# Gather or pair: 186 instead of 144 edge chunks of a graph layer built from an on-chip table, earlier and with larger offset loads

## The chip, the cores and the metric

The kernel runs on one core of one Trainium2 chip. The metric is the device time of one execution in microseconds; lower is better.

## What is computed

One layer of a graph network with a residual, all float32: N = 12500 nodes of D = 128 features, E = 200000 edges sorted by destination, H = 512.

```python
edge_index = jnp.stack([src, dst])
h = jnp.maximum(_layernorm(x, axis=-1), 0.0)
x = x + _L0_gnn_ref(h, edge_index, ...)
# _L0_gnn_ref(z, edge_index, ...):
msgs = z[src]
agg = jax.ops.segment_sum(msgs, dst, num_segments=n)
deg = jax.ops.segment_sum(jnp.ones((src.shape[0],), z.dtype), dst, num_segments=n)
agg = agg / jnp.maximum(deg, 1.0)[:, None]
h = jax.nn.relu(agg @ Wg + z @ Ws + bg)
h = jnp.tanh(h @ W1 + b1)
h = jnp.tanh(h @ W2 + b2)
return h @ W3 + b3
```

## The kernel before

**Set-up** (lines 282 to 400). The function that runs is `windowed`; `general` is a fallback for other graphs. x comes in pieces of ten tiles of 128 rows. Each piece is normalised: VectorE (DVE) sums and centres, ScalarE (ACT) squares (L270) and takes the root (L276), DVE scales (L280) into a tile `h`, and SP stores it to the row table `htab` in memory. In between, src and dst are turned by TensorE (PE) into columns (L340): `scol` holds the row numbers to gather, `dloc` the places of the destinations. `places` keeps, for every fourth chunk, the addresses of the rows of its 128 edges in a second table.

**Chunks.** The edges are 1563 chunks of 128. A chunk's 128 rows of h are multiplied by a one-hot matrix (L540 on DVE, for eight chunks at once, five buffers) and added into PSUM by PE (`add`, L695). The rows come in three ways:

- 80 chunks in ten groups are *raw*: POOL gathers rows of x (L217) before `htab` is there, and DVE normalises them (`centre`, four operations of 128x1024 a group) between the one-hots of the first hundred chunks.
- Most come by a *gather* of `htab`, one indirect DMA on POOL a chunk (L451), into a ring of 26 tiles (`AHEAD`).
- Of every fourth chunk some are made *by pairs* from a table on chip. `tab` (128 x 12544) holds h turned, one column a node. A chunk takes 64 operations, each of which reads two columns, whose places stand in registers, and writes their sum and the second of them (the one-hot is made to fit, L547). `lanes[0]` does this on ACT (L491, reported as L518), `lanes[1]` on DVE (L500). The offsets come into registers by a load (L461, TENSOR_LOAD) of `LOADS` = 16 numbers, that is eight pairs. PE then transposes the finished columns (`turn`, L505) and ACT copies them to a tile `turned`, which is added like a gathered one.

**`tab`** is filled in the loop: for each block of 512 nodes SP loads `htab` back (`own`, L746), PE transposes four tiles, ACT copies them into `tab` (`own_turned`, L754), one block every two chunks, 25 in all.

**Order.** PE, ACT and SP work in the order in which the program is written (`keep_in_program_order`); DVE's one-hots and pairs are placed by the same loop over chunks (L934). Its clock is `behind`, the number of gathered chunks added so far. `load_times` (L887) puts the pairs of a chunk on ACT 28 gathers ahead of its use, on DVE 36; `turns` (L901) puts transpose and copy 14 ahead. So everything that ACT does at a place in the loop that depends on PE waits until PE is there. The one-hot of a group of eight is written two groups ahead. The matrix layers of a finished block (512 nodes) are spread over the chunks that follow (`go_on`); from chunk 1312 on (`QUICK`) they follow a plan of when each gather lands.

**Which chunks.** `SHARES` = 72, 72 chunks for ACT and DVE are spread evenly over the slots (every fourth chunk from the fourth on) from `FROM` = 80 up to `ENDS` = 1480 and 1540. 1563 - 80 - 144 = 1339 chunks are gathered.

Of the kernel before, what the change touches and what calls it, by code (L numbers as in the profile page):

```python
# [22 lines left out]
F32 = mybir.dt.float32  # L23
# [8 lines left out]
P = 128  # L32
EPS = 1e-5
CPR = 16
BLK = 512
# [10 lines left out]
BEHIND = 2  # L46
EVERY = 4
AT = 3
SHARES = 72, 72
FROM, ENDS = 80, (1480, 1540)  # L50
MARGIN = 28
SUMS_AT, BANK = 1 << 25, 2048
AHEAD_OF_USE = 2
EDGE_BANK = 7
TOGETHER = 4
LOADS = 16

# [23 lines left out]
def windowed(ctx, tc, x, src, dst, Wg, Ws, bg, W1, b1, W2, b2, W3, b3, out, flag):  # L81
    nc = tc.nc
    N, D = x.shape
# [57 lines left out]
    blocks, n = [], 0  # L141
# [46 lines left out]
    ps_m = ctx.enter_context(tc.tile_pool(name="ps_m", bufs=4, space=PSUM))  # L188
# [5 lines left out]
    for t, a in ((rsrc, src), (rdst, dst)):  # L194
        a = a[RAW0 * P : RAW1 * P].rearrange("(u e) -> u e", u=NRAW)[:, : GRP * P]
# [18 lines left out]
    for g in range(NRAW):  # L214
        t = raws.tile([P, GRP, D], F32, name=f"raw{g}")
# [7 lines left out]
    ident = const.tile([P, P], F32, name="ident")  # L223
# [41 lines left out]
    def centre(pool, xt, k, stats, bufs=2):  # L265
        nc.vector.tensor_reduce(stats[:, 0], xt, AX.X, ALU.add)
        nc.vector.scalar_tensor_tensor(xt, spread(stats[:, 0], k), -1.0 / D, xt, op0=ALU.mult, op1=ALU.add)  # L267
        sq = (pool.tile([P, PIECE, D], F32, name="sq") if bufs > 1 else pool.tile([P, GRP, W_RAW], F32, name="ohr", bufs=1)[:, :, :D])[:, :k]
        if bufs > 1:
            nc.scalar.activation(sq, xt, AF.Square)  # L270
        else:
            nc.vector.tensor_tensor(sq, xt, xt, op=ALU.mult)
        nc.vector.tensor_reduce(stats[:, 1], sq, AX.X, ALU.add)
# [8 lines left out]
    with tc.tile_pool(name="ln", bufs=2) as ln:  # L282
# [80 lines left out]
        for i, (t0, k) in enumerate(pieces):  # L363
            xt = ln.tile([P, PIECE, D], F32, name="xt", bufs=3)
            whole = min(N - t0 * P, k * P) // P
            rest = min(N - t0 * P, k * P) - whole * P
            if rest:
                nc.vector.memset(xt[:, whole, :], 0.0)
            nc.sync.dma_start(xt[:, :whole, :], x[t0 * P : (t0 + whole) * P, :].rearrange("(t p) d -> p t d", p=P))
            if rest:  # L370
                nc.sync.dma_start(xt[:rest, whole, :], x[(t0 + whole) * P : N, :])
            if i == 1:
                indices("src", src, 0, keep_src)
            stats = ps_a.tile([P, BLK], F32, name="agg")[:, : 2 * k].rearrange("p (s t) -> p s t", s=2)
            xt = xt[:, :k]
            centre(ln, xt, k, stats)
            factors(stats)
            h = ln.tile([P, PIECE, D], F32, name="h", bufs=2)
            scale(h[:, :k], xt, k, stats)
            nc.sync.dma_start(htab[t0 * P : (t0 + k) * P, :].rearrange("(t p) d -> p t d", p=P), h[:, :k])  # L380


        number = sp.tile([NROW, CPR], F32, name="number")
# [50 lines left out]
    ml = ctx.enter_context(tc.tile_pool(name="ml", bufs=2))  # L434
# [11 lines left out]
    def sp_dma(*a):  # L446
        tc.keep_in_program_order(nc.sync.dma_start(*a))
# [10 lines left out]
    def offsets(lane, c, p0):  # L458
        r, q = divmod(c, CPR)
        kind = (mybir.EngineType.Activation, mybir.EngineType.DVE)[lane]  # L460
        loads, vs = nc.values_load_multi_w_load_instructions(  # L461
            places[r : r + 1, q // EVERY, p0 : p0 + LOADS], engines=[kind], min_val=TAB_AT,
            max_val=TAB_AT + (N - 1) * 4,
# [14 lines left out]
    def two(lane, c, p0):  # L478

        by_pair = columns[c].rearrange("p (t i) -> p i t", t=2)  # L480
        at_v = dict(offsets(lane, c, p0))
        for p in range(p0, p0 + LOADS, 2):
            a, b = (tab[:, bass.ds((at_v[q] - TAB_AT) // 4, 1)] for q in (p, p + 1))
            yield p, by_pair[:, p // 2], a, b

    def column_copies():
        for c in lanes[0]:
            columns[c] = ed.tile([P, P], F32, name="cols1", bufs=4)
            for p0 in range(0, P, LOADS):
                for p, to, a, b in two(0, c, p0):  # L490
# [4 lines left out]
    def column_pairs():  # L495
        for c in lanes[1]:
            columns[c] = ed.tile([P, P], F32, name="cols2", bufs=6)
            for p0 in range(0, P, LOADS):
                for p, to, a, b in two(1, c, p0):
# [241 lines left out]
                s = out  # L741
            nc.vector.tensor_tensor(out, s, rd[:, a0 - n : a1 - n], op=ALU.mult)

    owns, xss, stores = {}, {}, []

    def own(s):  # L746

        n0 = s * BLK
        k = -(-min(BLK, N - n0) // P)
        hb = ml.tile([P, BLK // P, D], F32, name="xb")  # L750
        sp_dma(hb[:, :k], htab[n0 : n0 + k * P, :].rearrange("(t p) d -> p t d", p=P))
        owns[s] = hb

    def own_turned(s):  # L754

        k = -(-min(BLK, N - s * BLK) // P)
        hb = owns.pop(s)
        pt = ps_m.tile([P, BLK // P, P], F32, name="pm")
        for t in range(k):
            pe.transpose(pt[:, t, :], hb[:, t, :], ident)  # L760
        act.copy(tab[:, s * BLK : s * BLK + k * P], pt[:, :k, :].rearrange("p t n -> p (t n)"))

    def own_part(b):

# [122 lines left out]
    def load_times(lane):  # L887
# [18 lines left out]
    def store(upto):  # L906
        while stores and stores[0][0] <= upto:
            sp_dma(*stores.pop(0)[1:])
# [11 lines left out]
            if w[1] is None:  # L920
                work.remove(w)

    nown = -(-N // BLK)
    own(0)
    own(1)
    own_turned(0)
    own(2)
    onehot(0)
    onehot(1)
    told_begins()  # L930
# [3 lines left out]
    for c in range(NCH):  # L934
        g = c // GRP
        at = c
        store(c - (SOON if c >= QUICK else LATE))
        if c % GRP == 0 and g + 2 < ngrp:
            onehot(g + 2)
            if raw((g + 2) * GRP):  # L940
                raw_scaled(((g + 2) * GRP - RAW0) // STEP)
            if g == 2 + NRAW + 2:
                worst = checked()
            if 2 <= g < 2 + NRAW:
                centre(ed, raw_rows[g - 2], GRP, raw_stats(g - 2), bufs=1)
            if g == 2 + NRAW + 5:
                factors(stats_raw)

        if c % (GRP // 2) == 0 and g + 2 < ngrp:
            copies, times = loading[1]  # L950
            while times and times[0] <= behind:
                times.pop(0)
                next(copies, 0)
        while c % GRP == GRP // 2 and counted < len(blocks) and reach[counted][-1] // GRP <= g + (c >= QUICK):
            count(counted)
            counted += 1
        while nxt < len(order) and nxt < behind + AHEAD:
            gather(order[nxt])
            nxt += 1
        if not raw(c) and c not in apart:  # L960
            behind += 1
            copies, times = loading[0]
            while times and times[0] <= behind:
                times.pop(0)
                next(copies, 0)
            while turns and turns[0][0] <= behind:
                turn(turns.pop(0)[1])
        if c >= QUICK:

            there = 7.5 + 1.251 * (NRAW * GRP + order.index(c)) if c not in apart else 0  # L970
            if c == QUICK:
                now = there - SPREAD
            while soonest() and max(now, soonest()[2]) < there:
                go_on(soonest())
            now = max(now, there) + 0.27
        add(c)

        lead = LEAD if c < QUICK else 2
        if done < len(blocks) and (c - lead if across[done] else c) >= reach[done][-1]:
            quick = reach[done][-1] + LEAD >= QUICK  # L980

            prev, older = (i if i >= 0 and reach[i][-1] + LEAD < QUICK else None for i in (done - 1, done - 2))
            older = None if quick and prev is None else older
            work.append([layers(done, prev, older), 0, 0, 0, quick and blocks[done][1] <= P])
            done += 1

        if c % TILE_EVERY == 1 and c // TILE_EVERY < NT:
            tallied(c // TILE_EVERY)
            if c // TILE_EVERY == NT - 1:
                outside(worst)  # L990
            if c // TILE_EVERY + EARLY < NT:
                seen(c // TILE_EVERY + EARLY)
        if c % 2 == 1 and c // 2 + 1 < nown:
            own_turned(c // 2 + 1)
            if c // 2 + 3 < nown:
                own(c // 2 + 3)
        if c < QUICK:
            if c % 2 == 0:
                go_on(work[0] if work else None)
                fetch_ahead(c)  # L1000
        if c == QUICK:
            for b, (_, n) in enumerate(blocks):
                if n < BLK:
                    own_part(b)
# [376 lines left out]
```

## Time and profile before

| | |
|---|---|
| median of three runs | 1805.02 us (1799.81, 1805.02, 1805.12) |
| profiled execution | 1800.16 us, span 1798.4 us |
| mean granted TensorE clock | 0.830 |
| PE busy | 1399.2 us (78%), 5410 matmuls |
| DVE busy | 1034.4 us (58%), 5580 instructions |
| ACT busy | 1534.3 us (85%), 5169 instructions |
| POOL busy | 1348.5 us (75%), 1428 instructions |

Busy shares are means over a span of three parts: a set-up of some 100 us, the loop, and an end in which the last blocks go through the layers. A row of a group reads: line, engine, operation, out<-in, count, then busy us, mean ns of one, idle us before it and who ended that. Operations overlap in their engine's pipeline, so the distance between starts, not the duration, is the price of one in a row of many. Register loads (TENSOR_LOAD) run on an engine's sequencer and are not counted as busy.

### The profile page before, as it was taken

The page shows a single profiled execution, that of the slowest core. Times are in us where ns is not written, and L with a number is a line of the kernel's source. Part 1 is how long each engine was busy: PE and PEld are TensorE (multiplying, and loading weights), DVE is VectorE, ACT ScalarE, POOL GpSimd, SP SyncE. Part 2 cuts the span into 40 slices and gives each one's busy share as a digit, 9 for nine tenths or more (in the row PEclk, how much of TensorE's full clock was granted, in tenths as well). Part 3 has the DMA queues.
Part 4 walks back from the last instruction along what each step waited for, and adds up shares of the span by engine and source line. Part 5 has one row for each costly group of instructions (what it writes and reads, how often), then busy time and mean ns, then how long its engine had stood idle before and what let it go on. Part 6 is the DMA issues. An engine that isn't in the chain of part 4 may idle for free.

```text
span 1798.4 us, 26668 instructions
## 1 busy us (share of the span) xinstructions
PE 1399.2 (78%) x5410; PEld 926.5 (52%) x5410; DVE 1034.4 (58%) x5580; ACT 1534.3 (85%) x5169; POOL 1348.5 (75%) x1428
## 2 busy tenths in 40 slices
PE   0047576878787888897888888787888888779998
PEld 0036454555455555555555555545555554555567
DVE  7965866666655656566565665556556655435400
ACT  1213999999999999999999999999999999998223
POOL 7777777777777777777777777777777777777774
PEclk9999999767887786877867868879787788778998
DMA  8954222222222222222222222222222222222221
GB/s 209 242 140 139 55 67 58 64 61 70 58 73 71 59 73 71 57 73 71 71 59 71 71 59 71 71 59 73 71 59 71 71 56 73 71 65 71 59 62 45
DMA packets 129832, 138.77 MB, mean 77 GB/s; under 512 B 30119, under 2 KB 106019, under 8 KB 129464
## 3 DMA queue, kind: packets, MB, share of 16 engines
q0 software_dynamic: 45408, 93.09, 19.9%
q1 hardware_dynamic: 80974, 40.37, 8.3%
q10 hardware_dynamic: 3276, 3.51, 0.7%
q14 instruction: 128, 1.05, 0.2%
q8 instruction: 46, 0.75, 0.2%
HBM read 123.84 MB, written 13.03 MB: 76 GB/s over the span
## 4 chain that ended last, share of the span: by engine, by line
ACT 29%; PE 25%; DMA 19%; issue 13%; POOL 9%; ACTq 4%; DVE 0%; DVEq 0%; POOLq 0%
ACT cols L518 25%; DMA rows<-htab,scol 19%; PE pm L441 17%; PE agg L441 6%; POOL rows L451 4%; POOL raw L217 4%; ACTq L461 4%; ACT h L518 3%; PE edge L441 2%; PE pm L444 1%; ACT turned L518 0%; ACT rd L521 0%; ACT o L521 0%; DVE cols L500 0%; DMA raw<-in_x_dram,rsrc 0%
## 5 line engine op out<-in xcount | busy, mean ns | idle before, releaser
L451 POOL DMA_INDIRECT rows<-htab,scol x1339 | 1267.8, 947 | 408.0 <-issue 226.7
L518 ACT ACTIVATE cols<-both_first,tab 128x2 f32<-128x2 f32 x4608 | 1351.2, 470 | 3.8 <-issue 1.9
L441 PE MATMUL pm<-h,w 128*128 128x512 f32 (+4 forms) x1344 | 795.0, 692 | 25.0 <-ACT h L518 20.5
L500 DVE SCALAR_TENSOR_TENSOR cols<-first_only,tab 128x2 f32<-128x2 f32 x4608 | 666.6, 218 | 250.4 <-issue 249.3
L441 PEld LDWEIGHTS agg<-oh,rows 128*128 128x128 f32 x1928 | 394.6, 253 | 426.8 <-DMA rows<-htab,scol 260.5
L441 PE MATMUL agg<-oh,rows 128*128 128x24 f32 x1928 | 398.7, 307 | 177.2 <-DMA rows<-htab,scol 172.2
L540 DVE TENSOR_TENSOR oh<-shared,dloc 128x192 f32<-128x192 f32 x186 | 65.5, 354 | 356.6 <-PE agg L441 211.0
L441 PEld LDWEIGHTS pm<-h,w 128*128 128x128 f32 x1344 | 243.6, 229 | 33.5 <-ACT h L518 22.4
L441 PEld LDWEIGHTS edge<-oh,rows 128*128 128x128 f32 x750 | 144.0, 233 | 164.8 <-DMA rows<-htab,scol 89.4
L441 PE MATMUL edge<-oh,rows 128*128 128x24 f32 x750 | 145.9, 289 | 63.3 <-DMA rows<-htab,scol 59.4
L518 ACT ACTIVATE h<-pm,b2c 128x512 f32<-128x512 f32 (+4 forms) x112 | 76.9, 689 | 51.6 <-PE pm L441 51.6
L217 POOL DMA_INDIRECT raw<-in_x_dram,rsrc x80 | 79.8, 998 | 25.6 <-issue 23.8
L587 DVE TENSOR_SCALAR_CACHE_REDUCE nearby<-nearby,parity 128x656 uint8<-128x656 uint8 x98 | 86.8, 886 | 0.0
L518 ACT ACTIVATE h<-pm,b1c 128x512 f32<-128x512 f32 (+4 forms) x112 | 76.6, 694 | 11.8 <-PE pm L441 11.2
L521 ACT COPY tab<-pm 128x512 f32<-128x512 f32 (+1 forms) x25 | 14.4, 577 | 68.1 <-PE pm L444 68.1
L340 PE MATMUL pm<-ident,idx_f 98*128 98x98 f32 x32 | 5.7, 373 | 82.5 <-DVE idx_f L334 54.4
L441 PEld LDWEIGHTS agg<-oh,turned 128*128 128x128 f32 x196 | 45.1, 258 | 36.6 <-issue 33.0
L444 PE MATMUL pm<-ident,cols 128*128 128x128 f32 x144 | 49.2, 342 | 10.7 <-ACT h L518 5.4
L518 ACT ACTIVATE turned<-pm 128x128 f32<-128x128 f32 x144 | 50.3, 349 | 7.4 <-PE pm L444 7.4
L740 DVE TENSOR_TENSOR mT<-agg,sums 128x136 f32<-128x136 f32 (+6 forms) x57 | 15.3, 272 | 71.3 <-PE agg L441 61.9
L441 PE MATMUL pm<-ident,h 128*128 128x128 f32 (+1 forms) x196 | 43.8, 309 | 14.4 <-ACT h L518 14.3
L270 ACT ACTIVATE sq<-xt 128x1280 f32<-128x1280 f32 (+3 forms) x11 | 12.7, 1153 | 44.6 <-DVE xt L267 35.4
(129 smaller groups left out, 850.8 us busy)
## 6 DMA issues: line engine op xcount, KB each, us to landing
rows<-htab,scol POOLq DMA_INDIRECT x1339
nearby<-bytes_at SPq DMA_DIRECT2D x98, 82.0 KB
xb<-htab SPq DMA_DIRECT2D x24, 256.0 KB
xb<-in_x_dram SPq DMA_DIRECT2D x23, 256.0 KB
out_dram<-o SPq DMA_DIRECT2D x23, 256.0 KB
xt<-in_x_dram SPq DMA_DIRECT2D x8, 640.0 KB
htab<-h SPq DMA_DIRECT2D x8, 640.0 KB
raw<-in_x_dram,rsrc POOLq DMA_INDIRECT x80
```

Source lines behind the costliest of these rows:

```text
L217: nc.gpsimd.indirect_dma_start(out=t[:, j, :], out_offset=None, in_=x, in_offset=bass.IndirectOffsetOnAxis(ap=rsrc[:, g, j : j + 1], axis=0),)
L270: nc.scalar.activation(sq, xt, AF.Square)
L441: tc.keep_in_program_order(nc.tensor.matmul(*a, **k))
L444: tc.keep_in_program_order(nc.tensor.transpose(*a, **k))
L451: nc.gpsimd.indirect_dma_start(out=r, out_offset=None, in_=htab, in_offset=bass.IndirectOffsetOnAxis(ap=scol[:, c : c + 1], axis=0),)
L461: loads, vs = nc.values_load_multi_w_load_instructions(places[r : r + 1, q // EVERY, p0 : p0 + LOADS], engines=[kind], min_val=TAB_AT, max ...
L500: last[:] = [tc.keep_in_program_order(nc.vector.scalar_tensor_tensor(to, first_only, a, b.to_broadcast([P, 2]), op0=ALU.mult, op1=ALU.subtract
L518: tc.keep_in_program_order(nc.scalar.activation(*a, **k))
L521: tc.keep_in_program_order(nc.scalar.copy(*a))
L540: newest[:] = [nc.vector.tensor_tensor(oh[:, :k, :w], lane[:, None, :w].to_broadcast([P, k, w]), dloc[:, g * GRP : g * GRP + k][:, :, None ...
L587: done = nc.vector.tensor_scalar(w, w, parity[:, t % 2 : t % 2 + 1], None, op0=ALU.is_equal, op1=ALU.add, accum_out=found[:, t : t + 1])
L740: nc.vector.tensor_tensor(out, s, t, op=ALU.add)
```

## The change

Four things.

- `tab` is filled in the set-up: right after a piece's `h` is stored, PE transposes its tiles and ACT copies them. `own` and `own_turned` and their reloads are gone.
- `FROM` is 30 instead of 80. Chunks by pairs begin with chunk 35 (DVE) and 39 (ACT) instead of 95 and 87, and their pairs stand in the order from the first gathered chunk on.
- `LOADS` is 32 instead of 16: one load feeds 16 pairs. A chunk has four loads instead of eight.
- `SHARES` is 76, 110 instead of 72, 72: 1563 - 80 - 186 = 1297 chunks are gathered. ACT makes 4864 pairs (4608 before), DVE 7040 (4608).

```diff
-SHARES = 72, 72
-FROM, ENDS = 80, (1480, 1540)
+SHARES = 76, 110
+FROM, ENDS = 30, (1480, 1540)
...
-LOADS = 16
+LOADS = 32
...
             nc.sync.dma_start(htab[t0 * P : (t0 + k) * P, :].rearrange("(t p) d -> p t d", p=P), h[:, :k])
+            for a in range(0, k, 4):
+                n = min(4, k - a)
+                p = ps_m.tile([P, 4, P], F32, name="pm")
+                for t in range(n):
+                    nc.tensor.transpose(p[:, t, :], h[:, a + t, :], ident)
+                nc.scalar.copy(tab[:, (t0 + a) * P : (t0 + a + n) * P], p[:, :n, :].rearrange("p t n -> p (t n)"))
...
-    def own(s):
...
-    def own_turned(s):
...
-    own(0)
-    own(1)
-    own_turned(0)
-    own(2)
...
-        if c % 2 == 1 and c // 2 + 1 < nown:
-            own_turned(c // 2 + 1)
-            if c // 2 + 3 < nown:
-                own(c // 2 + 3)
```

How this moves the instructions is shown at two places. The first is DVE between the statistics of the fourth raw group (`raw_128`) and the one-hot `oh_207` of chunks 64 to 71. Before:

```order
L266 TENSOR_REDUCE shared<-raw_128 128x8
L597 TENSOR_SCALAR degs<-found 128x4
L267 SCALAR_TENSOR_TENSOR raw_128<-shared,raw_128 128x1024
L598 RECIPROCAL degs<-degs 128x4
L272 TENSOR_TENSOR ohr<-raw_128 128x8x128
L273 TENSOR_REDUCE shared<-ohr 128x8
L540 TENSOR_TENSOR oh_207<-shared,dloc 128x192
```

The same place now (L506 are the pairs, L467 their loads, L546 the one-hot):

```order
L266 TENSOR_REDUCE shared<-raw_128 128x8
L604 RECIPROCAL degs<-degs 128x4
L267 SCALAR_TENSOR_TENSOR raw_128<-shared,raw_128 128x1024
L272 TENSOR_TENSOR ohr<-raw_128 128x8x128
L273 TENSOR_REDUCE shared<-ohr 128x8
L467 TENSOR_LOAD places
L506 SCALAR_TENSOR_TENSOR cols_3307<-first_only,tab 128x2 x16
L467 TENSOR_LOAD places
L506 SCALAR_TENSOR_TENSOR cols_3307<-first_only,tab 128x2 x16
L546 TENSOR_TENSOR oh_207<-shared,dloc 128x192
```

Two batches of 16 pairs, each behind its load, now stand between a raw group's statistics and the next one-hot; at other groups it is two or three. Ahead of the one-hot of chunks 112 to 119 stand 35 such batches; before, 25 of half the size.

The second place is ACT from the last piece of the set-up to its first pairs. Before:

```order
L270 ACTIVATE sq<-xt 128x1024
L276 ACTIVATE agg<-agg,eps 128x8
L521 COPY tab<-pm 128x512 x24
L521 COPY tab<-pm 128x256
L461 TENSOR_LOAD places
L518 ACTIVATE cols_1157<-both_first,tab 128x2 x8
```

Now (L386 are the copies into the table):

```order
L386 COPY tab<-pm 128x512
L270 ACTIVATE sq<-xt 128x1024
L386 COPY tab<-pm 128x512
L386 COPY tab<-pm 128x256
L276 ACTIVATE agg<-agg,eps 128x8
L386 COPY tab<-pm 128x512 x2
L467 TENSOR_LOAD places
L524 ACTIVATE cols_1196<-both_first,tab 128x2 x16
```

The 25 copies that stood between the set-up and the first pair are spread over the set-up; two of them follow its last root. Behind the copy `turned` of chunk 123, which stands at gather 97, ACT's order has 4442 pairs; in the order of before, 4490 stand behind the first `turned`.

More of the change, by code (lines that the diff above doesn't have):

```diff
@@ L742, in merged @@
             nc.vector.tensor_tensor(out, s, rd[:, a0 - n : a1 - n], op=ALU.mult)
-    owns, xss, stores = {}, {}, []
-    def own(s):
[L748 to L752, printed above, removed]
-    def own_turned(s):
[L756 to L761, printed above, removed]
+    xss, stores = {}, []
     def own_part(b):
@@ L921, in go_on @@
                 work.remove(w)
-    nown = -(-N // BLK)
-    own(0)
-    own(1)
-    own_turned(0)
-    own(2)
     onehot(0)
```

## The prediction

> **What bounds the kernel now.** I read the waits of POOL first (who was waited for: sum in us, times, longest in us).
>
> ```profile
> POOL rows L451 <- issue: 226.7, 744, 0.3
> POOL rows L451 <- DMA rows<-htab,scol: 75.2, 247, 0.3
> POOL rows L451 <- PE agg L441: 57.6, 189, 0.3
> ```
>
> No wait is longer than 0.3 us: POOL issues gathers back to back and is never stopped by a full ring of row tiles. The timeline gives the first gather, the pace of two neighbours, and the last:
>
> ```profile
> 107.27 0.95 POOL L451 DMA_INDIRECT rows<-htab,scol  x1 [0.30 <-issue]
> ...
> 1600.69 0.94 POOL L451 DMA_INDIRECT rows<-htab,scol  x1 [0.30 <-issue]
> 1601.94 0.95 POOL L451 DMA_INDIRECT rows<-htab,scol  x1 [0.30 <-issue]
> ...
> 1781.76 0.94 POOL L451 DMA_INDIRECT rows<-htab,scol  x1 [0.30 <-issue]
> ```
>
> So a gather takes 1.25 us, and the span (1798.4 us) ends 16.6 us after the last one begins. Then the busy time in three stretches (PE, PEld, DVE, ACT, POOL, granted clock, DMA share, GB/s):
>
> ```profile
> 174.00:1656.60 1482.60, 1214.44 (x4482) 783.10 (x4483) 880.05 (x5200) 1461.04 (x5025) 1121.22 (x1187) 0.80 0.25 66
> 1656.60:1798.40 141.80, 129.31 (x693) 96.66 (x691) 29.85 (x187) 39.08 (x95) 95.35 (x101) 0.92 0.23 61
> 110.00:174.00 64.00, 46.69 (x194) 39.91 (x194) 30.62 (x45) 13.88 (x25) 49.07 (x50) 1.00 0.53 147
> ```
>
> The first stretch runs from the first pair on ACT to the last. ACT is busy in 98.5% of it and idles 21.6 us. So two bounds stand side by side, gathers and ACT; and in the last 142 us a third, PE, at 91%.
>
> **The gathers.** 42 more chunks by pairs leave 1297 gathers. If all else kept up, the span would be 1798.4 - 42 x 1.25 = 1745.9 us. The first gather does not move: it stands behind the 80 raw gathers, and the row table it reads is in memory 11 us earlier, when SP's next load, which waited for it, is issued:
>
> ```profile
> 96.00 5.12 SPq L447 DMA_DIRECT2D xb<-htab  x3
> ```
>
> **The columns' table.** Its 24 reloads on SP, 98 transposes on PE and 25 copies on ACT leave the loop; transposes and copies now stand among the set-up's pieces.
>
> ```profile
> L521 ACT COPY tab<-pm 128x512 f32<-128x512 f32 (+1 forms) x25 | 14.4, 577 | 68.1 <-PE pm L444 68.1
> 173.97 32.98 ACT L518 ACTIVATE cols<-both_first,tab 128x2 f32<-128x2 f32 x118 [1.03 <-DVE oh L547]
> 206.86 0.25 ACT L518 ACTIVATE turned<-pm 128x128 f32<-128x128 f32 x1
> ```
>
> In the set-up DVE sets the pace and ACT has room, so the 14.4 us cost nothing there; without that cover they would lengthen the set-up, of which 11 us are hidden from the gathers. The table is then complete near 97 us instead of 173 us. This is not 75 us won. ACT works strictly in its order; a "turned" of chunk c stands 14 gathers ahead of c and waits for PE's transpose, which stands behind PE's additions up to there. ACT can only be as far as PE is.
>
> **ACT's sum.** One pair costs 32.98 / 118 = 0.2795 us, a chunk of 64 pairs 17.9 us, four more chunks 71.6 us. The 4608 pairs of before are 1288 of the 1461 us; 173 us are the rest (h, turned, copies). I start from the thirteenth turned in the new order, of chunk 123, which stands at gather 97 (counted from 0); 4442 of the 4864 pairs stand behind it. When its row is there:
>
> ```profile
> L451 POOL DMA_INDIRECT rows<-htab,scol x98 | 95.7, 977 | 29.9 <-issue 21.0 <-DMA rows<-htab,scol 5.5 <-PE pm L444 1.8
> ```
>
> This counts gathers from 107 to 232 us: the 98th is issued at about 231.5 and has landed at 234. Behind it: 4442 x 0.2795 = 1241.5 us, and the same rest, 173 (the few that have passed and 28 more turned, 0.25 us each at most, about cancel): 1415 us. ACT's last pair cannot end before 234 + 1415 = 1649 us. The same working on before gives 206.9 + 4490 x 0.2795 + 172 = 1634, where 1656.6 was measured: there ACT had 22 us to spare. The gathers alone would let the last pair (at gather 1187) come at 234 + 1090 x 1.25 = 1597 us. **So from here ACT is the bound, and the 52 us of the gathers are not to be had.**
>
> Loading 32 offsets at a time costs or saves ACT nothing: the 118 pairs ran without a break across some 15 loads of 1.0 us, and the eleven queued pairs found below last 3.1 us, more than a load of twice the size. PE gains 42 transposes of 0.34 us in the loop and loses 98 there, which comes out at nothing:
>
> ```profile
> L444 PE MATMUL pm<-ident,cols 128*128 128x128 f32 x144 | 49.2, 342 | 10.7 <-ACT h L518 5.4 <-ACT turned L518 3.4 <-issue 0.8
> L444 PE MATMUL pm<-ident,xb 128*128 128x128 f32 x98 | 26.9, 429 | 6.0 <-DMA xb<-htab 6.0
> ```
>
> **DVE's sum.** Three batches of eight pairs, their loads, loads of other sizes on PE's sequencer (8 registers behind a raw group, then 16), and a load of one register on DVE:
>
> ```profile
> 412.85 1.14 DVE L500 SCALAR_TENSOR_TENSOR cols<-first_only,tab 128x2 f32<-128x2 f32 x8 [0.99 <-issue]
> 414.33 1.14 DVE L500 SCALAR_TENSOR_TENSOR cols<-first_only,tab 128x2 f32<-128x2 f32 x8 [0.34 <-issue]
> 415.81 1.15 DVE L500 SCALAR_TENSOR_TENSOR cols<-first_only,tab 128x2 f32<-128x2 f32 x8 [0.33 <-issue]
> ...
> L461 DVEq TENSOR_LOAD <-places x3: 1126/1128/1130, 411.6 to 414.6; - x3
> ...
> L654 PEldq TENSOR_LOAD <-spots x1: 605/605/605, 990.3 to 990.3; - x1
> ...
> L654 PEldq TENSOR_LOAD <-spots x1: 1147/1147/1147, 996.5 to 996.5; - x1
> ...
> L1346 DVEq TENSOR_LOAD <-flag x1: 534/534/534, 1785.9 to 1785.9; - x1
> ...
> L500 DVE SCALAR_TENSOR_TENSOR cols<-first_only,tab 128x2 f32<-128x2 f32 x4608 | 666.6, 218 | 250.4 <-issue 249.3
> ```
>
> A batch comes every 1.48 us: 1.13 of load plus 0.35 to hand out eight pairs, which themselves start every (1.14 - 0.22) / 7 = 0.131. The load sets the pace. No row shows 32 registers. Upper bound: twice 16, 1.13 x 2 - 0.08 = 2.17 us, since 8 to 16 nearly doubles. Lower: the line from 1 to 16 on DVE, 0.04 us a register, 1.76 us. I take 2.17, by the rows nearest in size. A batch of 16 pairs is then 2.17 + 0.70 = 2.87 us (bounds 2.1, the pairs alone, and 2.96, two of before): 97% of before's price, for 38 more chunks.
>
> These batches now begin while DVE still has the raw rows' statistics to do, and the one-hots stand behind both.
>
> ```profile
> 91.17 1.21 DVE L280 SCALAR_TENSOR_TENSOR h<-xt,agg 128x1024 f32<-128x1024 f32 x1
> ...
> 85.37 2.85 PE L340 MATMUL pm<-ident,idx_f 98*128 98x98 f32 x16 [54.41 <-DVE idx_f L334]
> ...
> L273 DVE TENSOR_REDUCE shared<-ohr 128x8 f32<-128x1024 f32 x10 | 12.2, 1225 | 0.3
> L587 DVE TENSOR_SCALAR_CACHE_REDUCE nearby<-nearby,parity 128x656 uint8<-128x656 uint8 x98 | 86.8, 886 | 0.0
> L540 DVE TENSOR_TENSOR oh<-shared,dloc 128x192 f32<-128x192 f32 x186 | 65.5, 354 | 356.6 <-PE agg L441 211.0
> ```
>
> The last piece of the set-up is done at 92.4; the turning of dst (2.85 us on PE), now behind the pieces' transposes, its copies, the first one-hots and the row counts follow, some 13 us: DVE starts on pairs at about 105 (101 to 109). Ahead of the one-hot of chunks 112 to 119 stand 35 batches, 100.5 us; forty operations on raw rows, 12.2 us for ten, less overlap 46; seven tallies 6.2; one-hots and checks 12. That is 165 us: it is ready at 270. Its first row, gather 101, lands at 239. PE is **30 us late**. Before, 25 half-size batches (37 us) stood there, and DVE was early. DVE does not catch up soon: afterwards a chunk of pairs comes every 11.3 gathers, 14.1 us, and asks 11.5 us, beside some 2 us of other work (880 - 667 us in the stretch of 1483). The 26 row tiles cover 26 x 1.25 - 2.5 = 30 us, so the gathers just about run on; but ACT, tied to PE's place, has waited.
>
> **The end.** ACT's last pair: 234 + 30 + 1415 + 4 (waits for PE) = 1683 us; the 4 are a part of
>
> ```profile
> ACT h L518 <- PE pm L441: 16.0, 9, 3.9
> ```
>
> in the same stretch of before. Behind it stand 110 gathered rows, before 111 in 141.8 us with PE busy 129.3. With the rows already there PE no longer waits for gathers: 129 to 142, I take 131. Span 1814 us, with the 1.8 us around it 1816 against the profiled 1800.2: 0.9% slower. The three timed runs (1799.8, 1805.0, 1805.1) lie up to 5 us above the profiled one; for a median I add 1 us: **1817 us**.
>
> **Rivals.**
> *The load has a fixed part* (not slower). By the one-register row, 32 cost 1.76, a batch 2.46, 35 of them 86: late by 16, span 1800, time 1802. With the pairs alone as the pace, 2.1: late by 3, 1787, time 1789. It decides below 2.45 us a batch. For it: 534 ns for one register. Against: 605 for 8 beside 1147 for 16. The Trainium skill ("DMA: Bandwidth & Descriptors", Latency and other measured facts) gives tensor_load a floor of about 600 ns that unrolling spreads; added to 32 registers' share of the rest it would be an estimated 1.65 us, and a batch 2.35. The trace has loads below that floor.
> *The gathers stay the bound*: 1745.9, time 1748, if ACT could run further ahead than its turned lets it. Against: 98.5%.
> *The sequencer cannot hand out 16 pairs at once*: the next load waits until only eight are left, so a batch is 2.17 + 8 x 0.131 + 0.1 = 3.3 us, the one-hot 45 us late, beyond the ring: the gathers stop, the end is 1829 or later, and 440 such batches alone fill 1452 us of DVE: up to 1850. A row against it, on ACT:
>
> ```profile
> L461 ACTq TENSOR_LOAD <-places x1: 1020/1020/1020, 179.7 to 179.7; - x1
> ```
>
> 32 pairs stand ahead of this load, and by 179.7 some 21 had begun, (179.7 - 174.0) / 0.28: eleven were queued. The Trainium skill ("Advanced Engine Details and Errata", Engine Queue Depths) gives ScalarE and VectorE 8, which speaks for this rival; the trace shows more.
>
> **Chances.** Forecast 0.48 (1802 to 1828), fixed part 0.30 (1787 to 1803), gathers 0.08, queue 0.14. 0.3% of the time, 5 us, is about what a measurement tells from no change. Faster: gathers 0.08, over half of the fixed part 0.19, a little of the forecast 0.03: 0.30. Same: 0.10 of the fixed part, 0.08 of the forecast: 0.18. Slower: 0.52. Range 1781 to 1840; beyond it lie the gathers' case and the worse half of the queue's.
>
> **What would show it.** Right: places loads near 2.2 us on DVE; one-hots of chunks 56 to 112 the last to come for PE; ACT without idle time from 300 us on; its last pair near 1683; POOL with waits over 0.3 us. Wrong: loads under 1.8 us, ACT's last pair before 1660, POOL without waits.

## The result, and the profile after

The change makes the kernel slower by 6.5%, where I had forecast 0.7%; 1920 us lies outside my range of 1781 to 1840 us.

| | before | after |
|---|---|---|
| median | 1803.76 us (1799.81 to 1805.12) | 1920.16 us (1919.59 to 1920.61) |
| ratio, 95% interval | | 1.0645 (1.0629 to 1.066) |
| span of the profiled execution | 1798.4 us | 1918.2 us |
| first, last gather | 107.3, 1781.8 us | 106.1, 1881.3 us |
| last pair on ACT, on DVE | 1656.6, 1706.8 us | 1765.7, 1838.3 us |
| pairs on DVE, from first to last | 1533 us for 72 chunks | 1731 us for 110 chunks |

The waits of POOL after the change (who was waited for: sum in us, times, longest). Before, none was longer than 0.3 us:

```profile
POOL rows L457 <- issue: 210.0, 689, 0.3
POOL rows L457 <- PE agg L447: 197.1, 285, 15.9
POOL rows L457 <- PE edge L447: 74.6, 108, 14.5
```

The ring of 26 row tiles is now full time and again: POOL waits up to 15.9 us until TensorE (PE) has added a row. So the gathers are no longer the bound. Whom does PE wait for? Its waits:

```profile
PE pm L447 <- DVE mT L748: 166.5, 20, 15.0
PE agg L447 <- DVE oh L546: 89.5, 30, 10.9
PE pm L385 <- DVE h L280: 63.2, 9, 23.3
PE edge L447 <- DVE oh L546: 48.4, 15, 11.3
```

Three of the four, 304 us, are waits in the loop for VectorE (DVE): for one-hots, and for `mT`, the sums of a finished block, which DVE adds up and scales for the matrix layers. Before, PE's longest waits in the loop were 172.2 and 59.4 us for the gathered rows themselves. ScalarE (ACT), which I had forecast as the bound, in its turn waits for PE:

```profile
ACT h L524 <- PE pm L447: 139.7, 66, 12.3
ACT turned L524 <- PE pm L450: 39.8, 10, 6.6
```

The chain of work that ended last, by engine, confirms it. First before, where DVE held 0% of it, then now:

```profile
ACT 29%; PE 25%; DMA 19%; issue 13%; POOL 9%; ACTq 4%; DVE 0%; DVEq 0%; POOLq 0%
...
DVE 58%; issue 20%; ACT 7%; PE 7%; DVEq 4%; DMA 2%; ACTq 0%; SPq 0%; POOL 0%; POOLq 0%
```

And what does DVE wait for, if it is the bound at 70% busy? For its own next instruction. The group of pairs, and the register loads (min/median/max ns, first and last start):

```profile
L506 DVE SCALAR_TENSOR_TENSOR cols<-first_only,tab 128x2 f32<-128x2 f32 x7040 | 988.8, 217 | 459.1 <-issue 458.8
...
L467 DVEq TENSOR_LOAD <-places x440: 2097/2153/2883, 104.8 to 1833.7; - x147
```

A load of 32 offsets takes 2.15 us (I had taken 2.17), and 459 us pass in which DVE waits before pairs and for no other engine. (A batch is, from here on, one load and the 16 pairs that it feeds; its cycle is the time from its first pair to the first pair of the next batch.) A piece of DVE's timeline in the middle of the loop shows where:

```profile
908.44 2.21 DVE L506 SCALAR_TENSOR_TENSOR cols<-first_only,tab 128x2 f32<-128x2 f32 x16 [0.67 <-issue]
911.31 2.29 DVE L506 SCALAR_TENSOR_TENSOR cols<-first_only,tab 128x2 f32<-128x2 f32 x16 [0.66 <-issue]
914.43 2.20 DVE L506 SCALAR_TENSOR_TENSOR cols<-first_only,tab 128x2 f32<-128x2 f32 x16 [0.83 <-issue]
916.55 0.35 DVE L546 TENSOR_TENSOR oh<-shared,dloc 128x192 f32<-128x192 f32 x1
916.82 0.88 DVE L593 TENSOR_SCALAR_CACHE_REDUCE nearby<-nearby,parity 128x656 uint8<-128x656 uint8 x1
917.63 0.08 DVE L593 DVE_READ_ACCUMULATOR nearby<-nearby,parity 128x1 f32 x1
917.63 0.23 DVE L553 SCALAR_TENSOR_TENSOR oh<-shared,partner,oh 128x24 f32<-128x24 f32 x1
919.19 2.31 DVE L506 SCALAR_TENSOR_TENSOR cols<-first_only,tab 128x2 f32<-128x2 f32 x16 [1.32 <-issue]
```

The load between the last two batches stands in that second by itself:

```profile
L467 DVEq TENSOR_LOAD <-places x1: 2150/2150/2150, 916.9 to 916.9; - x1
```

Two batches that follow one another are 2.87 us apart (908.44 to 911.31), as forecast: the load runs under the pairs before it. Where a one-hot and its partner operation (L553, which needs the one-hot done) stand between, the load comes behind both on DVE's sequencer. The partner waits for the one-hot's semaphore, which comes at 916.90 when the one-hot ends; only then does the load begin. Of the 198 such places of the trace, 168 have the load's start 0.05 us behind the end of the instruction that was waited for. So the 2.15 us lie open but for what the tally (L593, which counts the edges of a tile of nodes) covers, and the cycle from 914.43 to 919.19 is 4.76 us.

Sorting all batches of the timeline by whether another DVE operation stands between them and the next: 225 cycles of 2.926 us without, 214 of 5.002 us with one, 1728.7 us together, 15.7 us a chunk. At the pace of the gathers a chunk of pairs is due every 14.1 us. Taken together, the 214 interrupted cycles are 444 us longer than as many undisturbed ones: 270 us of that are busy time of the operations in between, 157 us are DVE standing idle before the next pairs for longer than the 0.68 us of an undisturbed batch, and 17 us are waits for others.

### The profile page after: what moved, and what is told of

It reads as the page before. It is cut to its first block, busy times and chain, and to the rows that moved or that the text cites. A ratio compares the mean times of both kernels' runs of the same rounds, so it can differ in the third digit from the quotient of the medians.

```text
span 1918.2 us, 28953 instructions
## 1 busy us (share of the span) xinstructions
PE 1334.2 (70%) x5430; PEld 918.7 (48%) x5452; DVE 1348.0 (70%) x8054; ACT 1612.9 (84%) x5471; POOL 1308.8 (68%) x1386
## 3 DMA queue, kind: packets, MB, share of 16 engines
q14 instruction: 145, 1.19, 0.2%
## 4 chain that ended last, share of the span: by engine, by line
DVE 58%; issue 20%; ACT 7%; PE 7%; DVEq 4%; DMA 2%; ACTq 0%; SPq 0%; POOL 0%; POOLq 0%
DVE cols L506 44%; ACT cols L524 6%; PE pm L447 5%; DVEq L467 4%; DVE nearby L593 4%; DVE oh L546 2%; DMA xt<-in_x_dram 1%; DVE oh L553 1%; DVE mT L748 1%; ACT h L524 1%; DMA rows<-htab,scol 1%; DVE ohr L546 1%; DVE raw L280 1%; PE agg L447 1%; DVE h L280 1%
## 5 line engine op out<-in xcount | busy, mean ns | idle before, releaser
L457 POOL DMA_INDIRECT rows<-htab,scol x1297 | 1229.3, 948 | 547.2 <-issue 210.0
L524 ACT ACTIVATE cols<-both_first,tab 128x2 f32<-128x2 f32 x4864 | 1408.3, 415 | 12.8 <-issue 9.0
L506 DVE SCALAR_TENSOR_TENSOR cols<-first_only,tab 128x2 f32<-128x2 f32 x7040 | 988.8, 217 | 459.1 <-issue 458.8
L447 PE MATMUL pm<-h,w 128*128 128x512 f32 (+4 forms) x1344 | 772.2, 674 | 64.4 <-ACT h L524 33.2
L447 PE MATMUL agg<-oh,rows 128*128 128x24 f32 x1868 | 361.8, 300 | 125.3 <-DVE oh L546 89.5
L447 PEld LDWEIGHTS edge<-oh,rows 128*128 128x128 f32 x726 | 121.9, 209 | 121.8 <-issue 68.0
L447 PE MATMUL pm<-mT,wg 128*128 128x512 f32 (+4 forms) x56 | 48.2, 959 | 166.5 <-DVE mT L748 166.5
L447 PE MATMUL edge<-oh,rows 128*128 128x24 f32 x726 | 113.5, 258 | 48.4 <-DVE oh L546 48.4
L593 DVE TENSOR_SCALAR_CACHE_REDUCE nearby<-nearby,parity 128x656 uint8<-128x656 uint8 x98 | 86.3, 881 | 0.0
L546 DVE TENSOR_TENSOR oh<-shared,dloc 128x192 f32<-128x192 f32 x186 | 64.2, 345 | 11.8 <-PE edge L447 8.9
L385 PE MATMUL pm<-ident,h 128*128 128x128 f32 x98 | 23.3, 423 | 66.2 <-DVE h L280 63.2
L450 PEld LDWEIGHTS pm<-ident,cols 128*128 128x128 f32 x186 | 49.5, 266 | 36.8 <-ACT turned L524 26.3
```

The lines of the kernel that those rows point to most:

```text
L385: nc.tensor.transpose(p[:, t, :], h[:, a + t, :], ident)
L447: tc.keep_in_program_order(nc.tensor.matmul(*a, **k))
L450: tc.keep_in_program_order(nc.tensor.transpose(*a, **k))
L457: nc.gpsimd.indirect_dma_start(out=r, out_offset=None, in_=htab, in_offset=bass.IndirectOffsetOnAxis(ap=scol[:, c : c + 1], axis=0),)
L506: last[:] = [tc.keep_in_program_order(nc.vector.scalar_tensor_tensor(to, first_only, a, b.to_broadcast([P, 2]), op0=ALU.mult, op1=ALU.subtract
L524: tc.keep_in_program_order(nc.scalar.activation(*a, **k))
```

## The experiments

**Theory.** DVE is the bound from the first pair to the last, because loads lie open behind operations that wait, and 110 chunks cost it 15.7 us each. **Rivals:** ACT with 76 chunks, as I had forecast; the early crowd on DVE, whose lateness stays; the table in the set-up, or PE's granted clock, which after the change is 0.50 in a stretch where it was 1.00:

```profile
110.00:174.00 64.00, 34.42 (x116) 27.68 (x117) 54.68 (x276) 61.44 (x223) 48.76 (x51) 0.50 0.23 59
```

Two kinds of chip came up. Six runs (share72_2, load_ahead_2 and loads16_2 together, act66_2, from80_2 and mix_2 together) had a chip on which the kernel before takes 1803 to 1808 us; twelve had chips on which it takes 2145 to 2166 us. Verdicts on the 1920 rest on the first kind; the second is told at the end.

### DVE's share back to 72

```diff
-SHARES = 76, 110
+SHARES = 76, 72
```

> The same kernel as share72 (the changed kernel with 72 chunks on VectorE), again, because on the chip of the first four runs the kernel before itself took 2166 us, with breaks between instructions on every engine (ScalarE's pairs alone waited 165 us in 261 breaks), so that the bounds stood differently. Where the kernel before takes about 1804: by the theory (DVE's share is what costs) 1794 to 1815; if ScalarE's 76 chunks, the set-up or TensorE's clock cost the time, above 1880.

Measured: 1801.37 us against 1807.61, ratio 0.9966 (0.9951 to 0.998). POOL's list is that of before:

```profile
POOL rows L457 <- issue: 223.8, 734, 0.3
POOL rows L457 <- DMA rows<-htab,scol: 60.7, 199, 0.3
POOL rows L457 <- PE agg L447: 59.5, 195, 0.3
```

The table in the set-up, the early start and loads of 32 remain, and nothing of the 116 us does. Four gathers less make 5.0 us, and 6.2 were won. Neither ACT's 76 chunks nor the set-up nor the clock cost anything here; the clock is again 0.52 to 0.53 up to 300 us:

```profile
100.00:174.00 74.00, 34.33 (x115) 27.20 (x115) 62.62 (x270) 68.61 (x247) 56.19 (x59) 0.52 0.24 64
174.00:300.00 126.00, 76.61 (x258) 58.82 (x258) 99.09 (x473) 108.76 (x379) 96.12 (x99) 0.53 0.23 60
```

ACT's last pair ends at 1659 us; my sum had put its bound at 1649.

### ACT's share from 76 to 66

```diff
-SHARES = 76, 110
+SHARES = 66, 110
```

> The same kernel as act66 (66 chunks on ScalarE, 110 on DVE in loads of 32). Where the kernel before takes about 1805: by the theory (DVE is the bound, ScalarE follows) 1905 to 1930; by the rival (ScalarE is the bound) 1740 to 1800.

Measured: 1899.8 us, ratio 1.0542 (1.0524 to 1.0559) against 1802.97. 179 us of ACT's work gone bring 20 us. ACT is not the bound; what it has won it waits:

```profile
ACT h L524 <- PE pm L447: 272.6, 93, 18.1
```

It was 139.7 us. The 20 us, 5 more than the theory allowed, are on DVE too: its pairs take 1704 us instead of 1731. Ten partner operations have gone, and fewer batches are interrupted (206 of 4.944 us, 233 of 2.931).

### Pairs from chunk 80 on

```diff
-FROM, ENDS = 30, (1480, 1540)
+FROM, ENDS = 80, (1480, 1540)
```

> The same kernel as from80 (76 and 110 chunks, loads of 32, pairs from chunk 80 on). Where the kernel before takes about 1805: by the theory (DVE is the bound all along) 1915 to 1950; by the early crowd 1875 to 1890.

Measured: 1961.2 us, ratio 1.0875 (1.0857 to 1.0893). The early crowd was no loss: without it the time is 41 us longer, outside what either side had said. The pairs:

```profile
L506 DVE SCALAR_TENSOR_TENSOR cols<-first_only,tab x7040: 204/214/292, 107.2 to 1838.1; 128x2 f32<-128x2 f32 x196
...
L506 DVE SCALAR_TENSOR_TENSOR cols<-first_only,tab x7040: 200/213/291, 156.7 to 1881.0; 128x2 f32<-128x2 f32 x196
```

The first row is the changed kernel, the second this one. They begin 49.5 us later, take 1724 us instead of 1731, end 43 us later, and the rest (80 us) is the same. I had expected that leaving the raw rows' work ahead of them would win some 50 us back; it won 7. So here the later start counted almost in full.

### Loads of 16

```diff
-LOADS = 32
+LOADS = 16
```

> The same kernel as loads16 (the changed kernel with 16 offsets to a load), again, for the same reason. Where the kernel before takes about 1804: by the theory 667 x 1.47 + 213 x 2.9 to 3.4 = 1600 to 1705 us of batches against 1729, time 1800 to 1900; by the price of loading alone, or by the early crowd, 1910 to 1930.

Measured: 1846.69 us, ratio 1.0216 (1.0199 to 1.0233). Of the 116 us lost, 73 go with the size of the loads alone, although the same 14080 offsets are loaded in 880 pieces or in 440. Undisturbed batches show no difference (665 cycles of 1.490 us, twice that 2.98). The 214 interrupted ones take 3.105 us: a short load lies open by less. The idle time before the next pairs, over that of undisturbed batches, falls from 157 us in all to 39. The chain is now shared: DVE holds 36% of it, ACT 25%.

### Each load right behind the pairs before it

```diff
+    def after_load(op):
+        if loaded:
+            tc.add_manual_dep(
+                op.ins, loaded[0].ins.name,
...
+            for p in range(p0, p0 + LOADS, 2):
...
+            if i + 1 < len(batches):
+                at_v = dict(offsets(1, *batches[i + 1]))
+            yield
```

`after_load` holds back the one-hots, tallies and the operations of mT until the load has been issued. Loads of 32 and all instructions stay; 439 loads of 440 now follow pairs, before 226.

> The same kernel as load_ahead (each load of 32 right behind the pairs before it), again, for the same reason. On the chip of the first runs an interrupted batch took 2.31 us of gap behind its pairs, and the load began 1.56 us ahead of their end. Where the kernel before takes about 1804: by the theory (a load behind an instruction that waits lies open) an interrupted batch falls from 4.8 to about 4.3 us, 198 x 0.5 = 100 us less of DVE's 1729, time 1820 to 1860; if only the number of instructions counts, 1920 +- 10.

Measured: 1843.39 us, ratio 1.0198 (1.0179 to 1.0216): 77 us for an order of instructions. A place like the one above:

```profile
905.53 2.20 DVE L519 SCALAR_TENSOR_TENSOR cols<-first_only,tab 128x2 f32<-128x2 f32 x16
908.40 0.36 DVE L561 TENSOR_TENSOR oh<-shared,dloc 128x192 f32<-128x192 f32 x1 [0.67 <-PE edge L447]
908.67 0.89 DVE L609 TENSOR_SCALAR_CACHE_REDUCE nearby<-nearby,parity 128x656 uint8<-128x656 uint8 x1
909.49 0.08 DVE L609 DVE_READ_ACCUMULATOR nearby<-nearby,parity 128x1 f32 x1
909.49 0.24 DVE L569 SCALAR_TENSOR_TENSOR oh<-shared,partner,oh 128x24 f32<-128x24 f32 x1
909.64 0.28 DVE L620 TENSOR_SCALAR degs<-found 128x4 f32<-128x4 f32 x1
909.96 0.18 DVE L621 RECIPROCAL degs<-degs 128x4 f32<-128x4 f32 x1
910.05 2.17 DVE L519 SCALAR_TENSOR_TENSOR cols<-first_only,tab 128x2 f32<-128x2 f32 x16
...
L467 DVEq TENSOR_LOAD <-places x1: 2149/2149/2149, 906.2 to 906.2; - x1
```

The load begins at 906.2, while the pairs from 905.53 on still run, and ends 0.6 us after them; the pairs at 910.05 follow the last small operation without idle time. The cycle is 4.52 us with two operations more in it than the 4.76 of before. (The row names PE for the 0.67 us; by the rows it is the load, which the one-hot now stands behind.) Over all, 240 cycles of 4.457 and 199 of 2.903 us, 15.0 us a chunk. This is what shows the mechanism: the counts are the same, only where the load stands has changed.

The 77 us are not all that DVE could win by it, for something else stops the kernel here. The chain, and the busy time before and after 300 us (PE, PEld, DVE, ACT, POOL):

```profile
ACT 70%; PE 10%; DVE 6%; POOL 5%; ACTq 4%; issue 4%; DMA 1%; DVEq 0%; POOLq 0%
...
174.00:300.00 126.00, 40.15 (x182) 34.07 (x183) 106.57 (x503) 62.94 (x217) 77.35 (x79) 0.54 0.18 46
300.00:1710.40 1410.40, 1101.57 (x4324) 732.84 (x4324) 1082.39 (x6912) 1404.91 (x4851) 1019.79 (x1078) 0.76 0.25 64
```

DVE's share of the chain falls from 58% to 6%. ACT is busy in half of the time up to 300 us, while PE adds rows some 41 us after their gathers were issued (mean of gathers 80 to 119); from there to its last pair at 1710.4 it idles 5.5 us in all, and the end comes 130 us later. That is the path that I had forecast, ACT behind a late start, with 1683 and 131 us. DVE in its turn waits 135 us for PE from 110 us on, against 39 in the changed kernel, so part of its 15.0 us a chunk is waiting. On these chips no run takes chunks from ACT with the loads so placed and 110 on DVE; that ACT is the bound here is read from the trace alone.

### Fewer gathers after all

Loads of 16, right behind the pairs, 72 chunks on ACT and 100 on DVE; table in the set-up and early start as in the change.

```diff
-SHARES = 76, 110
+SHARES = 72, 100
...
-LOADS = 32
+LOADS = 16
```

> The same kernel as mix (72 chunks on ScalarE, 100 on DVE, loads of 16 right behind the pairs before them). On the chip with breaks it took 1.017 of the kernel before, and DVE still waited 345 us for its own loads and issues. Where the kernel before takes about 1805: if the gathers are the bound again 1760 to 1785; if DVE still is, 1785 to 1815.

Measured: 1769.66 us, ratio 0.9824 (0.9808 to 0.984): 1.8% faster than the kernel before, and faster than the changed one. 28 gathers fewer than before are 35 us, and 33 were won. POOL's waits are short again, and DVE waits for PE:

```profile
POOL rows L457 <- issue: 213.3, 700, 0.3
POOL rows L457 <- PE agg L447: 67.5, 218, 0.9
...
DVE oh L561 <- PE agg L447: 103.3, 46, 6.9
DVE oh L561 <- PE edge L447: 70.9, 25, 8.3
```

Here the granted clock was 1.00 up to 300 us, with the set-up of share72_2; in both the gathers ran on with no wait over 0.9 us:

```profile
174.00:300.00 126.00, 61.96 (x239) 52.19 (x239) 110.49 (x540) 88.22 (x305) 95.35 (x98) 1.00 0.22 56
```

### On the chips where the kernel before takes 2145 to 2166 us

Twelve runs of the same kernels, and of two others. The first is the kernel before with `SHARES = 76, 110` alone; the other is mix with 66 and 112 chunks.

| run | ratio, 95% interval |
|---|---|
| shares_only; _2; _3; _4 | 1.0123 (1.0101 to 1.0144); 1.0177 (1.0127 to 1.0228); 1.0175 (1.0139 to 1.021); 1.02 (1.0139 to 1.026) |
| mix | 1.0173 (1.0118 to 1.0228) |
| share72 | 1.0216 (1.019 to 1.0241) |
| mix_more; _2 | 1.0264 (1.0226 to 1.0302); 1.0301 (1.025 to 1.0352) |
| load_ahead | 1.0307 (1.027 to 1.0344) |
| loads16 | 1.0359 (1.0337 to 1.0381) |
| act66 | 1.0605 (1.0546 to 1.0664) |
| from80 | 1.0688 (1.0623 to 1.0752) |

> The kernel before with nothing changed but the shares, 76 and 110 chunks: table reloaded in the loop, pairs from chunk 80 on, loads of 16. Theory (DVE cannot do 110 chunks in the loop's time, however they are loaded): about 1600 us of batches that begin at 175 us instead of 105, so the last pair on DVE comes near 1775 and the end some 85 us later: 1860 (1830 to 1890). Rival, the cost sits in loads of 32, the early start or the table: 1760 to 1805.

> The changed kernel with 72 chunks on VectorE, as before the change, and 76 on ScalarE; table in the set-up, early start and loads of 32 stay. Theory (DVE's share is what costs): 288 batches, some 200 of them interrupted, are about 200 x 4.8 + 88 x 2.9 = 1215 us, far below the loop; the bound is the gathers again, 1335 of them: 107 + 1334 x 1.25 + 17 = 1792 span, time 1794, up to 1815 if the early lateness stays. Rival, ScalarE with its 76 chunks is the bound: stays above 1880. Rival, the set-up's transposes with TensorE's granted clock at 0.50 up to 256 us cost the time: stays above 1880.

> The changed kernel with 16 offsets to a load, all else as changed. Theory: VectorE (DVE) is the bound through the whole loop, since 110 chunks by pairs ask 15.7 us each where the gathers give 14.1, and half of that is loads that lie open behind one-hots, tallies and mT (213 of 439 batches take 4.8 us, not 2.9). With loads of half the size an interrupted batch of 8 pairs should take 4.8 - 1.0 (half of the load) - 1.0 (half of the pairs) = about 2.9 us, an undisturbed one 1.47 as before the change: 667 x 1.47 + 213 x 2.9 = 1600 us for all, about 130 less than the 1729 now; with TensorE and ScalarE then close behind, time 1800 to 1860. Rival, the price of loading alone (the sum of the loads counts, not where they lie open): 880 x 1.48 = 1302 against 440 x 2.89 = 1272, so no change: 1920 +- 10. Rival, the early crowd on DVE (the lateness of the first 300 us stays to the end): nothing is gained there either, about 1910.

> The changed kernel with each load of 32 offsets on VectorE put right behind the pairs before it, and one-hots, tallies and mT only behind the load (439 of 439 loads follow pairs, now 226); the same instructions, the same counts. Theory (a load that stands behind an instruction with a wait starts only when that instruction is handed out, and lies open for its 2.15 us): an interrupted batch falls from 4.8 to about 4.0 us (0.74 to hand out pairs, 2.15 of load, some 1.1 of one-hot, partner and the like), 198 x 0.8 = 160 us less of DVE's 1729; then DVE ends near 1690 to 1720 and the time is 1800 to 1850. Rival, only the number of instructions on DVE counts: 1920 +- 10. Rival, early crowd or TensorE's clock: 1900 to 1920.

> The changed kernel with 66 chunks on ScalarE instead of 76; 110 on DVE, loads of 32, early start and table stay. Theory (DVE is the bound, ScalarE only follows): ten chunks less on ScalarE, 179 us of its work, change nothing; the ten gathers more are hidden too: 1910 to 1930. Rival, ScalarE is the bound as I had forecast, and TensorE's and POOL's waits come from it: 1740 to 1800.

> The changed kernel (110 chunks, loads of 32, table in the set-up) with pairs from chunk 80 on, as before the change. Theory (DVE is the bound all along, 3.9 us a batch): DVE's pairs took from 107 to 1838 us, some 50 of it with raw rows' work between; begun 45 to 65 us later without that work they end at 1835 to 1855: 1915 to 1940, nothing gained. Rival, the early crowd on DVE (30 us late, kept to the end by ScalarE's order): with the crowd gone 1875 to 1890. Rival, TensorE's granted clock of 0.50 in the first 260 us: by the clock's row, unchanged if it stays at 0.50.

> A version put together from what the runs showed: the changed kernel with 72 chunks on ScalarE and 100 on DVE, loads of 16, each load right behind the pairs before it. By the theory DVE needs 800 batches: 600 undisturbed at 1.47 and 200 at 2.7 to 3.0 us, 1420 to 1480 us and waits, in the 1650 us of the loop, so that the gathers are the bound again: 1311 of them, 106.4 + 1310 x 1.2525 + 17 = 1764 span, 1766 (1760 to 1785). If DVE's other work still makes it the bound (15.0 us a chunk as with load_ahead_2): 107 + 1500 + 100 to 140 of tail, 1780 to 1800, for TensorE would lag again. If the table or the early start cost time by themselves: above 1800.

> The same kernel as shares_only (the kernel before with shares 76 and 110: table reloaded in the loop, pairs from chunk 80 on, loads of 16), again, because on that chip the kernel before itself took 2166 us. Where the kernel before takes about 1805: with loads of 16 and the early start DVE's pairs ran from 107 to 1763 us, 1656 us for 110 chunks, some 50 of it raw rows' work. Theory (DVE cannot do 110 chunks in the loop's time): from 174 on they need 1600 to 1656 us, end 1774 to 1830, and 80 us of tail: 1855 to 1910. Rival, DVE can take 110 chunks in loads of 16 and the rest comes from the early start, the table or TensorE's clock: 1760 to 1805.

> mix with 66 and 112 chunks instead of 72 and 100: six gathers less, 7.5 us. In mix_2 DVE waited 174 us for TensorE at one-hots, 17 us for each of ten chunks more; twelve chunks more ask some 12 x 14 = 168 us. If that slack is enough: 1762 (1758 to 1768). If DVE becomes the bound again: 1775 to 1800.

shares_only_3 and shares_only_4 repeat shares_only, and mix_more_2 repeats mix_more, with the same expectations in short. None of the times in microseconds came true, since they were reckoned from a kernel of 1805. The six kernels that ran on both kinds of chip stand in the same order on both: mix, share72, load_ahead, loads16, act66, from80, though the intervals of some neighbours overlap. But share72, 0.3% faster there, is 2.2% slower here, and mix 1.7%. Why that is can be read in part. The first gather of share72 and, second, of shares_only, which has the set-up of before:

```profile
162.23 0.95 POOL L457 DMA_INDIRECT rows<-htab,scol  x1 [58.45 <-DVE dloc L359]
...
123.54 0.94 POOL L451 DMA_INDIRECT rows<-htab,scol  x1 [19.54 <-DVE oh L540]
```

On these chips the table in the set-up puts off the first gather by 39 us (on the others it came 1 us earlier), which is most of share72's 44 us, and of the 49 us by which loads16 lies above shares_only (the same shares and loads). It is not the early start: from80, which like shares_only leaves the pairs until chunk 80, has its first gather at 160.2 us. The loop has breaks on the engines as well: PE idled 206 us in share72 with nobody to wait for, and 5 in share72_2, and ACT's pairs alone waited in share72 (first row) and share72_2 (second)

```profile
ACT cols L524 <- issue: 165.1, 261, 1.7
...
ACT cols L524 <- issue: 7.3, 8, 1.8
```

with the same instructions, and with the pairs of a row 0.279 us apart on both. What makes the breaks was not found. For shares_only, which ran on no other kind of chip, this leaves open whether 110 chunks in loads of 16 alone would cost some 50 us there, as the theory says; here they cost 1.2 to 2%, less than the theory's 3 to 5%, and not nothing, as its rival had it. How far the share can grow past 100 stays open as well.

## Why the prediction was wrong

- **The gathers** (1745.9 if all else kept up; the first one does not move): the first came at 106.1, forecast as unmoved from 107.3. The price held where they were the bound: share72_2 and mix_2 lie within 2 us of the kernel before on their chip less 1.25 us for each gather saved.
- **The columns' table costs nothing in the set-up**: right by share72_2. On the other kind of chip it was not.
- **ACT's sum**: 1649 us as its lower bound held (1659 in share72_2). "So from here ACT is the bound" did not: act66_2 took 179 us from it and won 20. It is what shows once DVE's loads are out of the way: in load_ahead_2 ACT idles 5.5 us from 300 us to its last pair (the forecast's own sign of being right), in the changed kernel 79.
- **The load of 32 at 2.17 us, the batch at 2.87**: measured 2.15, and 2.93 for a batch followed by a batch. (The sum that I gave, 1.13 x 2 - 0.08, makes 2.18.) The fixed-part rival (under 2.45) is out. So is the queue rival: its 3.3 us for all batches do not show, as the load begins 1.57 us ahead of the end of the pairs before it (mean of 226 undisturbed batches), when most often eleven of the sixteen have not begun: (1.57 - 0.22) / 0.131, and the last one. The limit of 8 that the Trainium skill gives ("Advanced Engine Details and Errata", Engine Queue Depths) is not seen here.
- **The one-hot of chunks 112 to 119 ready at 270, 30 us late**: it ended at 276.0, and its first row, gathered from 235 on, was there at about 237.5: 38 us late. Right in kind, and 8 us short in size.
- **"DVE does not catch up soon: afterwards a chunk of pairs comes every 11.3 gathers, 14.1 us, and asks 11.5 us, beside some 2 us of other work". This step failed.** The 11.5 were 11.7 (4 x 2.926). The other work was taken at its busy time, 2 us. It costs 4.0: 214 interruptions of 5.002 - 2.926 = 2.08 us each, 444 us over 110 chunks. 2.5 of the 4.0 are busy time, the raw rows' work with it, and 1.4 are loads that lie open, a term that the sum did not have. Together 15.7 against 14.1, so that DVE never catches up; without the open loads it would be 14.3, next to the gathers' pace. PE's distance behind the gathers stays at 24 to 38 us (means over 40 gathers each, from 208 us to the end), held there by the ring of 26 tiles, which stops POOL; the gathers then go at DVE's pace. 440 batches took 1731 us where my price, 13.5 us a chunk, made 1485.
- **The end** (ACT's last pair 1683, 131 us behind it): ACT's came at 1765.7, but it was no longer the last; DVE's came at 1838.3, and 80 us followed. That the change came out slower, as I had said it would, is luck as far as the path goes: the forecast's lateness behind ACT is there, but the time was set by DVE.

The trace of before held a warning that I did not read. I quoted three batches in a row, without anything between. The next ones in its timeline:

```profile
415.81 1.15 DVE L500 SCALAR_TENSOR_TENSOR cols<-first_only,tab 128x2 f32<-128x2 f32 x8 [0.33 <-issue]
416.86 0.35 DVE L540 TENSOR_TENSOR oh<-shared,dloc 128x192 f32<-128x192 f32 x1
417.13 0.89 DVE L587 TENSOR_SCALAR_CACHE_REDUCE nearby<-nearby,parity 128x656 uint8<-128x656 uint8 x1
417.94 0.09 DVE L587 DVE_READ_ACCUMULATOR nearby<-nearby,parity 128x1 f32 x1
417.94 0.24 DVE L547 SCALAR_TENSOR_TENSOR oh<-shared,partner,oh 128x24 f32<-128x24 f32 x1
418.48 1.21 DVE L500 SCALAR_TENSOR_TENSOR cols<-first_only,tab 128x2 f32<-128x2 f32 x8 [0.30 <-issue]
```

Here the interruption costs 2.67 - 1.48 = 1.19 us, and the load of 1.13 us, which begins at 417.3, is all but hidden under the tally and the partner operation. One of 2.15 us in its place leaves a further microsecond open, which is what the row at 919.19 shows (1.32 instead of 0.30).

**What is shown and what is not.** Shown by runs: that DVE's share is what costs (share72_2), that in the changed kernel ACT and the early start do not (act66_2, from80_2), that the size and the place of the loads each carry some 75 of the 116 us (loads16_2, load_ahead_2; no run of 110 chunks on these chips has both, so how far the two overlap is open). That the sequencer stands at the partner's semaphore is read from the trace's times (0.05 us in 168 of 198 places), and load_ahead_2 agrees with it. Not shown by a run: what makes the 42 to 45 us that loads16_2 and load_ahead_2 still lie above share72_2. For load_ahead_2 the trace points at ACT and its late start, and not at DVE.

## What to carry to other kernels

Price a step that runs on an engine's sequencer where it is interrupted, not only where it repeats: a register load behind an instruction that waits for the one before it begins when that wait is over. What covered a load of 1.13 us left a microsecond of one of 2.15 open. Put such a load ahead of the operations that wait, and make it no longer than what covers it. An engine can be the bound at 70% busy; the sign is that its idle time is put down to its own issue, while the others wait for it. And when a bound is taken away, look whom the kernel waits for next before counting what is left against the first.

## What the runs showed of the hardware that was not expected

- A register load of 32 on DVE costs nearly twice one of 16: 2.153 and 1.121 us (medians of 440 and 880). Where the instruction ahead of it waits, it begins 0.05 us after that wait ends (168 of 198 places).
- ACT hands out a steady number of pairs ahead: in the kernel before, twelve loads in a row, from 177.5 to 202.0 us, each begin with eleven pairs handed out and not begun. They come every 2.23 us, the time of eight pairs, though a load takes 1.02. That points to a limit near eleven; no run tests it.
- PE's granted clock between 110 and 300 us was near 0.5 (0.50 to 0.61 in stretches of 30 to 64 us) in the changed kernel and share72_2 and 1.0 in mix_2, all with the same set-up. It changed no time where the gathers were the bound: over the four runs of mix_2 the mean granted clock was 0.77, 0.78, 0.84 and 0.85, and the times lie between 1767.9 and 1773.0 us. What sets it was not looked into.
- Chips differ by a fifth on this kernel (1803 to 1808 against 2145 to 2166 us), and a change can be a gain on one and a loss on the other (mix: 0.982 and 1.017).
